# Waits kept per tile at pool borders, and images stored once for gathers by rows of taps

## The chip, the cores and the metric

The kernel runs on one core of one Trainium2 chip. The metric is the device time of the whole program in microseconds (us). Three runs of the kernel before took 10018.24, 10019.67 and 10020.51 us; the median is 10019.67. A profile is one execution recorded by the hardware profiler. Its engines are PE (matrix multiplication; PEld is its loading of weights), DVE (vector), ACT (activation functions), POOL (general) and SP, which here issues the data transfers (DMAs). Each engine works through its own list of instructions in order and waits on semaphores where an instruction needs another engine's work or a DMA.

## The reference

The input is 4 images of 128 channels and 64 x 64 pixels, float32. Four layers, each added to its input, follow a normalization:

```python
x = x + L0(_gn(x))      # two depthwise convolutions, patch order, selective scan
x = x + L1(_gn(x))      # 3 x 3 convolution, 128 to 128 channels
t = tokens(x)
t = t + L2_attn(_ln_t(t));  t = t + L2_ffn(_ln_t(t))   # 16 heads of 8, softmax; 64 experts
t = t + L3_attn(_ln_t(t));  t = t + L3_ffn(_ln_t(t))   # linear attention; 64 experts
```

Layer 0 begins with the part that the change touches. A depthwise convolution has one 3 x 3 filter for each channel:

```python
feat = _gelu(_dwconv2d(x, conv1_w, conv1_b))
ca = sigmoid(relu(feat.mean((2, 3)) @ ca1_w.T) @ ca2_w.T)
feat = _gelu(_dwconv2d(feat * ca[:, :, None, None], conv2_w, conv2_b))
scores = 0.7 * sigmoid(head(feat)) + 0.3 * sigmoid(10 * var(x, axis=1))
idx = argsort(-patch_mean(scores))          # 256 patches of 4 x 4 pixels
```

The pixels are put in that order of patches, a position code is added, and the sequence of 4096 tokens goes through a normalization, a projection to 256 channels, a causal convolution, and a scan with 16 states per channel (h = dA * h + dBx, y = sum of h * C). The result is projected back and put back in image order.

## The kernel before

**Layers 0 and 1** (`layers01`, from L268). `in_order(b)` prepares image b: it loads it, normalizes it by groups (`groupnorm_fill`, ACT at L216) into `xp`, a 66 x 66 image with a border of zeros, and runs the first depthwise convolution into `fp`, the second over `fp`, then scores, sort and the ordered sequence. Depthwise convolutions run on PE (`convolved`, whose matmuls carry the line L91 of the helper `mm`). One product takes 96 rows: 32 channels times the three vertical taps ky, so that PE sums the vertical taps, and three products at shifted columns sum the horizontal ones. Four groups of 32 channels make a chunk of 8 image rows. The rows of `under`, the operand, are channel and ky: SBUF holds channels on partitions, so the image goes through DRAM. `stored` (L443) writes it to `image_d`, with three copies of each channel shifted by one row, and `gather` (L453) reads a chunk's 96 x 4 rows with one DMA of 792 KB. `image_d[0]` takes `xp` and `image_d[1]` takes `fp`, each in two halves, one half being 12 DMAs of 264 KB. `staged` starts a chunk's gather a set number of turns ahead of its product (`first`), and each `under` has two buffers.

Image 0 is prepared alone. Then `scan` goes through 32 chunks of the four sequences, 16 slots each, and takes one turn of the other work per slot: `in_order(1)` beside image 0's scan and so on, and beside the last one the putting back and layer 1's convolution (`end`). A slot has on DVE a product (L900) and two scans (L911), on ACT two exponentials (L907, `decay`), on POOL the product with C (L915, `hs<-hs,c_sb`), and SP loads C for it (L869, `c_sb<-c_d`). The order of the instructions on all five engines is the one that the program writes (`manual_schedule`); `later` puts an instruction at the end of the turn. `conv` results are read by ACT (gelu, L130), in order with `decay`.

In the sort, two comparisons per image need a mask of which patch comes before which; it is computed anew each time (L581, DVE).

**Layer 2** (`layer2_attention`, L1103). For each image: `prepare` (head features, queries, keys, values through DRAM), `attention` (scores on PE, exponential on ACT at L1534, sums and products on PE, DVE and POOL), then `feed_forward`, which runs beside the next image's `prepare` and ends with the stores `xd<-x` (L1667). Attention ends with the store of `around_d` (L1436), and feed_forward begins with the load of `den` (L1567). Then x is loaded (L2072); **`expert_ffn`** (L1700, gate first: `gateT`, `gate_ps`), **`layer3_attention`** (L1928, first product `ln_xc`) and `expert_ffn` again follow, and x is stored.

**Pools.** Tiles come from pools that are opened and closed with `with`: layer 2 opens `l2_mid` and `l2_ps` for prepare and feed_forward, closes them, and opens `l2_work`, `l2_pssc`, `l2_psctx`, `l2_psacc` for attention, on the same bytes. When a pool is opened on bytes of closed ones, its first use waits for all users of those pools, engines and DMAs. All DMAs named here are issued by SP in program order.

Of the kernel before, what the change touches and what calls it, by code (L numbers as in the profile page):

```python
# [9 lines left out]
F32 = mybir.dt.float32  # L10
# [3 lines left out]
ALU = mybir.AluOpType  # L14
AX = mybir.AxisListType
PSUM = bass.MemoryType.PSUM
# [253 lines left out]
def layers01(K, xd, dpool, w, w1):  # L270
# [7 lines left out]
    SLOTS = 2 * NG  # L278
    TURNS_END = 53
    with ExitStack() as ctx:  # L280
        pool = lambda name, bufs, **kw: ctx.enter_context(tc.tile_pool(name=name, bufs=bufs, **kw))
        cst = pool("l0_const", 1)
        big = pool("l0_big", 1)
        small = pool("l0_small", 1)
# [138 lines left out]
        def in_order(b, made, work, psum):  # L423
# [10 lines left out]
            sm = small.tile([P, 256], F32, name="sm")  # L434
            unders, kept, squares, features, xls = {}, {}, {}, {}, {}

            def stored(img, i, half):


                n = HW // 2 * (HW + 2)  # L440
                for g in range(4):
                    for ky in range(3):
                        nc.sync.dma_start(  # L443
                            out=image_d[i][g, 32 * ky : 32 * ky + 32, n * half : n * half + n],
                            in_=img[32 * g : 32 * g + 32, HW // 2 * half + ky : HW // 2 * (half + 1) + ky, :].rearrange(
                                "p y x -> p (y x)"
                            ),
                        )
# [118 lines left out]
            def sort():  # L567
                yield from wait(6)
                sp = K.bank(psum, [P, 256], "sm_ps")
                mm(sp, share.to_broadcast([P, P]), sm)  # L570
                later(nc.vector.tensor_copy, sm, sp)
                yield from wait(2)
                beats = []
                for h in range(2):
                    dg = small.tile([P, P], F32, name="dg")
                    nc.vector.tensor_tensor(dg, sm[:, h * P : (h + 1) * P], K.ident, ALU.mult)
                    cl = small.tile([P, 1], F32, name="cl")
                    nc.vector.tensor_reduce(cl, dg, AX.X, ALU.add)

                    before = small.tile([P, 256], F32, name="before")  # L580
                    nc.vector.scalar_tensor_tensor(before, K.col, K.row[:, h : h + 1], ones256, ALU.is_gt, ALU.mult)  # L581
                    eq = small.tile([P, 256], F32, name="eq", tag="rank_eq")
                    nc.vector.scalar_tensor_tensor(eq, sm, cl, before, ALU.is_equal, ALU.mult)
                    bt = small.tile([P, 256], F32, name=f"beats{h}")
                    nc.vector.scalar_tensor_tensor(bt, sm, cl, eq, ALU.is_lt, ALU.add)
                    beats.append(bt)
                    yield
                yield
                rp = K.bank(psum, [P, 256], "rank_ps")
                for h in range(2):  # L590
# [438 lines left out]

        seqs = []  # L1030
        with (
            tc.tile_pool(name="l0_first", bufs=2) as work,
            tc.tile_pool(name="l0_ps", bufs=8, space=PSUM) as psum,
        ):
            for K.slot, _ in enumerate(in_order(0, seqs, work, psum)):
                K.flush()
            K.flush()
        with (
            tc.tile_pool(name="l0_prep", bufs=1) as prep,
            tc.tile_pool(name="l0_scan", bufs=2) as work,  # L1040
            tc.tile_pool(name="l0_ps", bufs=3, space=PSUM) as psum,
            tc.tile_pool(name="l0_psbc", bufs=1, space=PSUM) as psbc,
            tc.tile_pool(name="l0_psex", bufs=2, space=PSUM) as psex,
            tc.tile_pool(name="l0_psy", bufs=1, space=PSUM) as psy,
            tc.manual_schedule(
                engines={
                    mybir.EngineType.PE,
                    mybir.EngineType.DVE,
                    mybir.EngineType.Activation,
                    mybir.EngineType.Pool,  # L1050
                    mybir.EngineType.SP,
                }
            ),
        ):
# [11 lines left out]
        with (  # L1066
            tc.tile_pool(name="l0_last", bufs=2) as work,
            tc.tile_pool(name="l0_ps", bufs=8, space=PSUM) as psum,
        ):
            for _ in end(NB - 1, seqs[NB - 1], work, psum):  # L1070
                K.flush()
# [32 lines left out]
def layer2_attention(K, xd, dpool, w):  # L1104
# [4 lines left out]
    BT = NTT // NJ  # L1109
    scale = 1.0 / math.sqrt(HD)  # L1110
    with ExitStack() as ctx:
        pool = lambda name, bufs, **kw: ctx.enter_context(tc.tile_pool(name=name, bufs=bufs, **kw))
        cst = pool("l2_const", 1)
        keep = pool("l2_keep", 2)

# [39 lines left out]
        with tc.tile_pool(name="l2_ps0", bufs=1, space=PSUM) as ps0:  # L1155
# [516 lines left out]
        past = None  # L1672
        for b in range(NB + 1):
            with (
                tc.tile_pool(name="l2_big", bufs=1) as big,
                tc.tile_pool(name="l2_two", bufs=2) as two,
            ):
                with (
                    tc.tile_pool(name="l2_mid", bufs=2) as work,
                    tc.tile_pool(name="l2_ps", bufs=8, space=PSUM) as psum,  # L1680
                ):
                    parts = list(feed_forward(b - 1, past, work, psum)) if b > 0 else []
                    if b < NB:
# [4 lines left out]
                    break  # L1688
                past = keep.tile([P, NTT, NH], F32, name="dsum")
                with (  # L1690
                    tc.tile_pool(name="l2_work", bufs=2) as work,
                    tc.tile_pool(name="l2_pssc", bufs=3, space=PSUM) as pssc,
                    tc.tile_pool(name="l2_psctx", bufs=1, space=PSUM) as psctx,
                    tc.tile_pool(name="l2_psacc", bufs=1, space=PSUM) as psacc,
                    tc.manual_schedule(
                        engines={mybir.EngineType.PE, mybir.EngineType.DVE, mybir.EngineType.Pool}
                    ),
# [4 lines left out]
def expert_ffn(K, xs, w, tag):  # L1702
# [8 lines left out]
    NG = NE // GE  # L1711
    NHC = HID // P
    with ExitStack() as ctx:
        pool = lambda name, bufs, **kw: ctx.enter_context(tc.tile_pool(name=f"{tag}_{name}", bufs=bufs, **kw))
        cst = pool("const", 1)
        wts = pool("wts", 2)
        tok = pool("tok", 1)
# [209 lines left out]
def layer3_attention(K, xs, w):  # L1927
# [1 line left out]
    nc, tc, mm = K.nc, K.tc, K.mm  # L1929
    HD = 16  # L1930
    with ExitStack() as ctx:
        pool = lambda name, bufs, **kw: ctx.enter_context(tc.tile_pool(name=name, bufs=bufs, **kw))
        cst = pool("l3_const", 1)
        big = pool("l3_big", 2)
        work = pool("l3_work", 2)
# [119 lines left out]
@with_exitstack  # L2055
def kernel(ctx: ExitStack, tc: tile.TileContext, w: dict, out: bass.AP):
    nc = tc.nc
    cpool = ctx.enter_context(tc.tile_pool(name="const", bufs=1))
    dpool = ctx.enter_context(tc.tile_pool(name="dram", bufs=1, space=bass.MemoryType.DRAM))
    K = Common(tc, cpool)  # L2060

    def of(prefix):
# [5 lines left out]
    xpool = ctx.enter_context(tc.tile_pool(name="x", bufs=1))  # L2068
    xs = []
    for b in range(NB):  # L2070
        t = xpool.tile([P, L], F32, name=f"x{b}")
# [61 lines left out]
```

## Time and profile before

| | before |
|---|---|
| three runs, median | 10019.67 us |
| the profiled execution | 10014.33 us |
| its span, first to last instruction | 10012.5 us |
| PE busy | 8755.8 us (87%) |
| DVE busy | 7222.2 us (72%) |
| ACT busy | 7414.1 us (74%) |
| POOL busy | 4804.1 us (48%) |
| granted PE clock, mean | 0.916 |
| bytes by DMA | 669.38 MB, 67 GB/s |

Times in the profile count from the span's start. Roughly: 0 to 241 us prepares image 0, to 2740 is the scan, to about 2980 the end of layer 1 and layer 2's beginning, to about 8890 layer 2, to 9261 its experts, to 9649 layer 3's attention, then its experts. A busy share over the whole span is an average over these stages; the prediction therefore goes by stages. A line of a timeline shows start, length, engine, line of the kernel and operation, output and inputs, count, and in brackets how long the engine was idle before and what ended it. A line of the waits shows who waited, for what, the total, how many times, and the longest. On SP a DMA's length is that of its issue, not of the transfer; SP also stands at a DMA when the queue behind it is full.

### The profile page before, as it was taken

What the parts mean: (1) busy time and instruction counts of PE and PEld (TensorE: products, weight loads), DVE (VectorE), ACT (ScalarE), POOL (GpSimd) and SP (SyncE); (2) the same over time, 40 slices, a digit from 0 to 9 for tenths busy, and PEclk for the clock granted to TensorE, in tenths of its full rate; (3) what the DMA queues carried; (4) which work ended last, traced back from release to release, by engine and by line L of the source; (5) the groups of instructions that cost most, each with busy time, mean ns of one, the idle gap of its engine ahead of it and who ended that gap; (6) DMA issues with size and microseconds to landing.
All of it is one profiled execution on the core that took longest, in us unless ns stands there. A gap on an engine that the chain in (4) does not pass through costs nothing.

```text
span 10012.5 us, 187862 instructions
## 1 busy us (share of the span) xinstructions
PE 8755.8 (87%) x74074; PEld 3353.2 (33%) x74074; DVE 7222.2 (72%) x7883; ACT 7414.1 (74%) x10669; POOL 4804.1 (48%) x3175
## 2 busy tenths in 40 slices
PE   5687888889859999979999979999979999967767
PEld 1122222235433333333333333333333333323433
DVE  1779797998738888848888858888758888743463
ACT  2666766654439999969999969999969999941531
POOL 0567586775525555545555545555545555420000
PEclk9787887889979999989999989999989999978888
DMA  5634536222221211141211141211141111133004
GB/s 127 150 88 101 134 79 152 69 73 81 74 70 37 41 39 39 30 115 38 39 39 39 29 115 39 39 38 39 29 115 39 38 39 39 33 100 118 2 18 152
DMA packets 578291, 669.38 MB, mean 67 GB/s; under 512 B 113592, under 2 KB 369664, under 8 KB 570240
## 3 DMA queue, kind: packets, MB, share of 16 engines
q1 hardware_dynamic: 577408, 657.36, 27.1%
q8 instruction: 584, 9.57, 0.4%
q14 instruction: 299, 2.45, 0.1%
HBM read 446.84 MB, written 143.13 MB: 59 GB/s over the span
## 4 chain that ended last, share of the span: by engine, by line
PE 45%; DVE 4%; DMA 2%; ACT 2%; POOL 1%; issue 1%; SPq 1%; DVEq 0%; POOLq 0%; ACTq 0%
PE ctx_ps L91 20%; PE acc_ps L91 10%; PE score L91 8%; PE ln_xc L91 1%; DMA w<-in_L_ffn_weight 1%; PE ln_var L91 1%; PE hid_ps L91 1%; PE kv L91 1%; PE tok_t L1829 0%; PE ln_var L121 0%; PE pool L91 0%; PE ans_ps L91 0%; DVE ctx L1468 0%; PE o_ps L91 0%; SPq L1210 0%
## 5 line engine op out<-in xcount | busy, mean ns | idle before, releaser
L1534 ACT ACTIVATE ex<-score 128x1024 f32<-128x1024 f32 x5120 | 4927.9, 1037 | 176.0 <-PE score L91 90.2
L91 PE MATMUL ctx_ps<-ex,qt 128*32 128x512 f32 x20480 | 2736.5, 606 | 19.8 <-DVE ctx L1468 19.8
L1483 POOL TENSOR_TENSOR folded<-ex 128x1024 f32<-128x1024 f32 x512 | 1224.2, 2391 | 2124.0 <-ACT ex L1534 1866.1
L1540 DVE STREAM_TRANSPOSE turned<-ex 128x1024 f32<-128x1024 f32 x1536 | 1885.9, 1228 | 351.5 <-ACT ex L1534 279.1
L1516 DVE STREAM_TRANSPOSE turned<-ex 128x1024 f32<-128x1024 f32 x1532 | 1843.0, 1203 | 0.0
L91 PE MATMUL acc_ps<-turned,turned_v 128*32 128x256 f32 x24576 | 1769.4, 379 | 3.0 <-DVE turned L1546 3.0
L911 DVE TENSOR_TENSOR_SCAN hs<-decay,carry,hs 128x512 f32<-128x512 f32 x1024 | 1245.8, 1266 | 248.2 <-ACT decay L907 234.9
L91 PE MATMUL score<-queries,keys 32*128 32x512 f32 x10240 | 1333.6, 497 | 64.4 <-POOL queries L1218 35.8
L91 PEld LDWEIGHTS acc_ps<-turned,turned_v 128*32 128x32 f32 x24576 | 800.8, 110 | 1476.5 <-issue 1327.2
L915 POOL TENSOR_TENSOR hs<-hs,c_sb 128x1024 f32<-128x1024 f32 x512 | 1207.5, 2358 | 108.9 <-DMA c_sb<-c_d 66.5
L907 ACT ACTIVATE decay<-dt,a_neg 128x512 f32<-128x512 f32 x1024 | 693.0, 689 | 662.5 <-DVE hs L911 653.0
L91 PEld LDWEIGHTS score<-queries,keys 32*128 32x128 f32 x10240 | 512.1, 182 | 1160.4 <-ACT ex L1534 801.8
L1346 POOL TENSOR_TENSOR turned_v<-v,quarter 128x1024 f32<-128x1024 f32 x256 | 612.5, 2393 | 266.3 <-PE acc_ps L91 221.8
L91 PE MATMUL y_ps<-hs,pair 128*64 128x512 f32 x2048 | 664.0, 776 | 27.0 <-POOL hs L915 26.9
L1484 POOL TENSOR_TENSOR quarters<-folded 128x512 f32<-128x512 f32 x512 | 658.0, 1285 | 40.1
L91 PEld LDWEIGHTS ctx_ps<-ex,qt 128*32 128x32 f32 x20480 | 406.5, 108 | 655.4 <-issue 599.3
L900 DVE TENSOR_TENSOR hs<-dtx,b_ps 128x2048 f32<-128x2048 f32 x256 | 580.5, 2267 | 55.1 <-PE b_ps L91 29.8
L91 PE MATMUL b_ps<-dbc,state 32*64 32x512 f32 x1024 | 339.6, 745 | 224.5 <-DVE hs L900 224.4
L1534 ACT ACTIVATION_READ_ACCUMULATOR ex<-score 128x1 f32 x2048 | 437.7, 214 | 0.0
L914 POOL COPY carry<-hs 128x2 f32<-128x2 f32 x512 | 98.1, 192 | 700.1 <-DVE hs L911 673.9
L1468 DVE COPY ctx<-ctx_ps 128x512 f32<-128x512 f32 x256 | 176.9, 691 | 329.2 <-PE ctx_ps L91 323.5
L91 PE MATMUL conv<-under,deep 96*32 96x512 f32 x1536 | 217.9, 708 | 136.6 <-DMA under<-image_d 128.3
(371 smaller groups left out, 9156.9 us busy)
## 6 DMA issues: line engine op xcount, KB each, us to landing
c_sb<-c_d SPq DMA_DIRECT2D x512, 128.0 KB
queries<-head_d SPq DMA_DIRECT2D x1024, 64.0 KB
keys<-head_d SPq DMA_DIRECT2D x1024, 64.0 KB
under<-image_d SPq DMA_DIRECT2D x64, 792.0 KB
dt<-dt SPq DMA_DIRECT2D x128, 256.0 KB
dtx<-dtx SPq DMA_DIRECT2D x128, 256.0 KB
v<-value_d SPq DMA_DIRECT2D x1024, 32.0 KB
w<-in_L_ffn_weight SPq DMA_DIRECT2D x32, 1024.0 KB
```

The costliest lines, as they stand in the source:

```text
L91: self.nc.tensor.matmul(out, lhsT, rhs, start=start, stop=stop)
L900: nc.vector.tensor_tensor(hs, dtx2, bb.unsqueeze(1).to_broadcast([P, NQ, CH]), ALU.mult)
L907: nc.scalar.activation(ex, dt2[:, q, :], AF.Exp, scale=a_neg[:, q, g : g + 1])
L911: nc.vector.tensor_tensor_scan(hs[:, q, :], decays[q - 2 * i], hs[:, q, :], carry[:, g, q : q + 1], ALU.mult, ALU.add)
L915: nc.gpsimd.tensor_tensor(hs[:, two, :], hs[:, two, :], cs.unsqueeze(1).to_broadcast([P, 2, CH]), ALU.mult)
L1346: nc.gpsimd.tensor_tensor(t, v.unsqueeze(2).to_broadcast([P, 4 * BT, 4, HD]), quarter.unsqueeze(1).to_broadcast([P, 4 * BT, 4, HD]), ALU.mult,
L1468: nc.vector.tensor_copy(u, cps)
L1483: nc.gpsimd.tensor_tensor(hs, exs[:, :, 0], exs[:, :, 1], ALU.add)
L1484: nc.gpsimd.tensor_tensor(qs, hs[:, :, 0 : CH // 2], hs[:, :, CH // 2 :], ALU.add)
L1516: nc.vector.transpose(*upright)
L1534: nc.scalar.activation(ex, sps[p], AF.Exp, scale=scale, accum_out=sums[:, t : t + 1] if summed else None)
L1540: nc.vector.transpose(*upright)
```

## The change

There are three edits.

1. Every pool is opened with `reuse_waits="tile"`. A tile on reused bytes then waits for the users of earlier tiles on its own bytes (in PSUM, its own bank) and not for all users of the closed pools. Outside layer 0 the instructions and their order on each engine stay the same.
2. `image_d` holds the bordered image once: 128 channels of 66 x 66. `stored` writes a quarter of it (17, 16, 16 and 17 rows) with one DMA from 128 partitions, and `gather` takes three DMAs of 264 KB, one per ky, each to 32 partitions. Per image that is 8 stores and 48 gathers in place of 48 and 16, and 2.23 MB written for each of `xp` and `fp` in place of 6.49 MB. Quarters of `xp` are stored after fills 3, 5 and 7 and after the last, those of `fp` after every second chunk.
3. The two masks of the sort are computed once, at setup.

In the diff only pools of one kind are shown once; all the others get the same argument.

```diff
     SLOTS = 2 * NG
     TURNS_END = 53
     with ExitStack() as ctx:
-        pool = lambda name, bufs, **kw: ctx.enter_context(tc.tile_pool(name=name, bufs=bufs, **kw))
+        pool = lambda name, bufs, **kw: ctx.enter_context(tc.tile_pool(reuse_waits="tile", name=name, bufs=bufs, **kw))
         cst = pool("l0_const", 1)
         big = pool("l0_big", 1)
         small = pool("l0_small", 1)
 ...
         state = cst.tile([32, DS], F32, name="state")
         nc.vector.tensor_scalar(state, K.col[0:32, 8 : 8 + DS], row32[0:32], None, ALU.is_equal)
         c_d = dpool.tile([2, DS, CH], F32, name="c_d")
-        image_d = [dpool.tile([4, 96, HW * (HW + 2)], F32, name=f"image_d{i}") for i in range(2)]
+        image_d = [dpool.tile([P, (HW + 2) * (HW + 2)], F32, name=f"image_d{i}") for i in range(2)]
         y_d = [dpool.tile([P, L], F32, name=f"y_d{b}") for b in range(NB - 2)]
 
         pair = cst.tile([P, 64], F32, name="pair")
 ...
         deep2 = depthwise(w["conv2_w"], "deep2")
         rect = lambda t: t.rearrange("p (y x) -> p y x", x=HW)
         ones256 = K.ones[:, 0:1].to_broadcast([P, 256])
+        befores = [small.tile([P, 256], F32, name=f"before{h}", bufs=1) for h in range(2)]
+        for h in range(2):
+            nc.vector.tensor_scalar(befores[h], K.col, K.row[:, h : h + 1], None, ALU.is_gt)
 
         def image(b):
             t = big.tile([P, L], F32, name="xb", tag="mid")
 ...
             sm = small.tile([P, 256], F32, name="sm")
             unders, kept, squares, features, xls = {}, {}, {}, {}, {}
 
-            def stored(img, i, half):
-
-
-                n = HW // 2 * (HW + 2)
-                for g in range(4):
-                    for ky in range(3):
-                        nc.sync.dma_start(
-                            out=image_d[i][g, 32 * ky : 32 * ky + 32, n * half : n * half + n],
-                            in_=img[32 * g : 32 * g + 32, HW // 2 * half + ky : HW // 2 * (half + 1) + ky, :].rearrange(
-                                "p y x -> p (y x)"
-                            ),
-                        )
+            def stored(img, i, q):
+
+
+                lo, hi = 16 * q + 1 if q else 0, 16 * q + 17 if q < 3 else HW + 2
+                nc.sync.dma_start(
+                    out=image_d[i][:, lo * (HW + 2) : hi * (HW + 2)], in_=img[:, lo:hi].rearrange("p y x -> p (y x)")
+                )
 
             def gather(i, c):
                 n = 8 * (HW + 2)
                 t = unders[c] = work.tile([96, 4, n], F32, name="under", bufs=2)
-                nc.sync.dma_start(out=t, in_=image_d[i][:, :, n * c : n * c + n].rearrange("g q f -> q g f"))
+                for ky in range(3):
+                    at = (8 * c + ky) * (HW + 2)
+                    nc.sync.dma_start(
+                        out=t[32 * ky : 32 * ky + 32],
+                        in_=image_d[i][:, at : at + n].rearrange("(g q) f -> q g f", q=32),
+                    )
 
             def even():
                 while K.slot % 2:
 ...
 
             for c in range(NCH):
                 fill(c)
-                if c == 6:
-                    stored(xp, 0, 0)
+                if c in (3, 5, 7):
+                    stored(xp, 0, c // 2 - 1)
                 yield
             fp = kept["fp"] = big.tile([P, HW + 2, HW + 2], F32, name="fp", tag="mid")
             nc.gpsimd.memset(fp[:, 0, :], 0.0)
 ...
             nc.gpsimd.memset(fp[:, 1 : HW + 1, 0:1], 0.0)
             nc.gpsimd.memset(fp[:, 1 : HW + 1, HW + 1 : HW + 2], 0.0)
             yield
-            stored(xp, 0, 1)
+            stored(xp, 0, 3)
 
             def first_stored(c):
-                if c in (4, 7):
-                    stored(fp, 1, c // 5)
+                if c % 2:
+                    stored(fp, 1, c // 2)
 
             yield from even()
             yield from staged(NCH, 2, lambda c: gather(0, c), None, None, first, None, first_stored)
 ...
                     cl = small.tile([P, 1], F32, name="cl")
                     nc.vector.tensor_reduce(cl, dg, AX.X, ALU.add)
 
-                    before = small.tile([P, 256], F32, name="before")
-                    nc.vector.scalar_tensor_tensor(before, K.col, K.row[:, h : h + 1], ones256, ALU.is_gt, ALU.mult)
                     eq = small.tile([P, 256], F32, name="eq", tag="rank_eq")
-                    nc.vector.scalar_tensor_tensor(eq, sm, cl, before, ALU.is_equal, ALU.mult)
+                    nc.vector.scalar_tensor_tensor(eq, sm, cl, befores[h], ALU.is_equal, ALU.mult)
                     bt = small.tile([P, 256], F32, name=f"beats{h}")
                     nc.vector.scalar_tensor_tensor(bt, sm, cl, eq, ALU.is_lt, ALU.add)
                     beats.append(bt)
 ...
             with (
-                tc.tile_pool(name="l2_big", bufs=1) as big,
-                tc.tile_pool(name="l2_two", bufs=2) as two,
+                tc.tile_pool(reuse_waits="tile", name="l2_big", bufs=1) as big,
+                tc.tile_pool(reuse_waits="tile", name="l2_two", bufs=2) as two,
             ):
 ...
```

More of the change, by code (lines that the diff above doesn't have):

```diff
@@ L1031, in layers01 @@
         with (
-            tc.tile_pool(name="l0_first", bufs=2) as work,
-            tc.tile_pool(name="l0_ps", bufs=8, space=PSUM) as psum,
+            tc.tile_pool(reuse_waits="tile", name="l0_first", bufs=2) as work,
+            tc.tile_pool(reuse_waits="tile", name="l0_ps", bufs=8, space=PSUM) as psum,
         ):
@@ L1038, in layers01 @@
         with (
[L1039 to L1044, printed above, removed]
+            tc.tile_pool(reuse_waits="tile", name="l0_prep", bufs=1) as prep,
+            tc.tile_pool(reuse_waits="tile", name="l0_scan", bufs=2) as work,
+            tc.tile_pool(reuse_waits="tile", name="l0_ps", bufs=3, space=PSUM) as psum,
+            tc.tile_pool(reuse_waits="tile", name="l0_psbc", bufs=1, space=PSUM) as psbc,
+            tc.tile_pool(reuse_waits="tile", name="l0_psex", bufs=2, space=PSUM) as psex,
+            tc.tile_pool(reuse_waits="tile", name="l0_psy", bufs=1, space=PSUM) as psy,
             tc.manual_schedule(
@@ L1066, in layers01 @@
         with (
-            tc.tile_pool(name="l0_last", bufs=2) as work,
-            tc.tile_pool(name="l0_ps", bufs=8, space=PSUM) as psum,
+            tc.tile_pool(reuse_waits="tile", name="l0_last", bufs=2) as work,
+            tc.tile_pool(reuse_waits="tile", name="l0_ps", bufs=8, space=PSUM) as psum,
         ):
@@ L1111, in layer2_attention @@
     with ExitStack() as ctx:
-        pool = lambda name, bufs, **kw: ctx.enter_context(tc.tile_pool(name=name, bufs=bufs, **kw))
+        pool = lambda name, bufs, **kw: ctx.enter_context(tc.tile_pool(reuse_waits="tile", name=name, bufs=bufs, **kw))
         cst = pool("l2_const", 1)
@@ L1154, in layer2_attention @@
         nc.vector.tensor_copy(biases[:, 1:2], b2)
-        with tc.tile_pool(name="l2_ps0", bufs=1, space=PSUM) as ps0:
+        with tc.tile_pool(reuse_waits="tile", name="l2_ps0", bufs=1, space=PSUM) as ps0:
             bp = ps0.tile([P, 2], F32, name="bias_ps")
@@ L1674, in layer2_attention @@
             with (
-                tc.tile_pool(name="l2_big", bufs=1) as big,
-                tc.tile_pool(name="l2_two", bufs=2) as two,
+                tc.tile_pool(reuse_waits="tile", name="l2_big", bufs=1) as big,
+                tc.tile_pool(reuse_waits="tile", name="l2_two", bufs=2) as two,
             ):
                 with (
-                    tc.tile_pool(name="l2_mid", bufs=2) as work,
-                    tc.tile_pool(name="l2_ps", bufs=8, space=PSUM) as psum,
+                    tc.tile_pool(reuse_waits="tile", name="l2_mid", bufs=2) as work,
+                    tc.tile_pool(reuse_waits="tile", name="l2_ps", bufs=8, space=PSUM) as psum,
                 ):
@@ L1690, in layer2_attention @@
                 with (
[L1691 to L1694, printed above, removed]
+                    tc.tile_pool(reuse_waits="tile", name="l2_work", bufs=2) as work,
+                    tc.tile_pool(reuse_waits="tile", name="l2_pssc", bufs=3, space=PSUM) as pssc,
+                    tc.tile_pool(reuse_waits="tile", name="l2_psctx", bufs=1, space=PSUM) as psctx,
+                    tc.tile_pool(reuse_waits="tile", name="l2_psacc", bufs=1, space=PSUM) as psacc,
                     tc.manual_schedule(
@@ L1713, in expert_ffn @@
     with ExitStack() as ctx:
-        pool = lambda name, bufs, **kw: ctx.enter_context(tc.tile_pool(name=f"{tag}_{name}", bufs=bufs, **kw))
+        pool = lambda name, bufs, **kw: ctx.enter_context(tc.tile_pool(reuse_waits="tile", name=f"{tag}_{name}", bufs=bufs, **kw))
         cst = pool("const", 1)
@@ L1931, in layer3_attention @@
     with ExitStack() as ctx:
-        pool = lambda name, bufs, **kw: ctx.enter_context(tc.tile_pool(name=name, bufs=bufs, **kw))
+        pool = lambda name, bufs, **kw: ctx.enter_context(tc.tile_pool(reuse_waits="tile", name=name, bufs=bufs, **kw))
         cst = pool("l3_const", 1)
@@ L2057 @@
     nc = tc.nc
-    cpool = ctx.enter_context(tc.tile_pool(name="const", bufs=1))
-    dpool = ctx.enter_context(tc.tile_pool(name="dram", bufs=1, space=bass.MemoryType.DRAM))
+    cpool = ctx.enter_context(tc.tile_pool(reuse_waits="tile", name="const", bufs=1))
+    dpool = ctx.enter_context(tc.tile_pool(reuse_waits="tile", name="dram", bufs=1, space=bass.MemoryType.DRAM))
     K = Common(tc, cpool)
@@ L2067 @@
     layer2_attention(K, xd, dpool, of("L2_attn_"))
-    xpool = ctx.enter_context(tc.tile_pool(name="x", bufs=1))
+    xpool = ctx.enter_context(tc.tile_pool(reuse_waits="tile", name="x", bufs=1))
     xs = []
```

## The prediction

> **What bounds the kernel now.** I read the page first. It shows an execution of 10014.33 us with a span of 10012.5, so 1.8 us lie around the span; the median of the runs, 10019.67, is 5.3 above it. I sum against 10014.33 and add the 5.3 at the end. PE is the busiest at 87%, but the average hides stages, so the busy time by windows comes next (columns: length, then busy time of PE, PEld, DVE, ACT, POOL, clock, DMA share, GB/s):
>
> ```profile
> 0.00:241.00 241.00, 123.60 (x654) 45.48 (x654) 35.58 (x102) 64.53 (x100) 24.90 (x41) 0.91 0.54 132
> 1000.00:1200.00 200.00, 158.93 (x717) 43.15 (x718) 139.61 (x109) 142.77 (x184) 114.23 (x85) 0.87 0.69 155
> 1200.00:2740.00 1540.00, 1300.96 (x4572) 520.14 (x4570) 1321.06 (x1122) 899.85 (x1219) 1039.87 (x787) 0.85 0.35 87
> ```
>
> In the first 241 us (image 0 alone) no engine is busy more than half. In the scan DVE is the fullest, but in the stretch with an image's convolutions it drops to 70%. The list of waits names what is missing:
>
> ```profile
> DVE hs L911 <- ACT decay L907: 234.9, 106, 18.1
> ...
> PE conv L91 <- DMA under<-image_d: 128.3, 17, 40.6
> ```
>
> Then the timeline. Image 0 (SPq is SP issuing DMAs; the bracket is idle time before a line and what ended it):
>
> ```profile
> 35.45 27.89 SPq L443 DMA_DIRECT2D image_d<-xp  x24
> ...
> 72.37 7.95 PE L91 MATMUL conv<-under,deep 96*32 96x512 f32 x48 [40.63 <-DMA under<-image_d]
> ...
> 98.70 12.44 SPq L443 DMA_DIRECT2D image_d<-fp  x11
> ...
> 120.45 5.23 PE L91 MATMUL conv<-under,deep 96*32 96x512 f32 x24 [11.67 <-DMA under<-image_d]
> ```
>
> PE waits for 24 stores, later for 12 more that sit ahead of two gathers on SP. In the scan the same stores hold a gather, PE and ACT wait, and DVE stands:
>
> ```profile
> 480.86 13.74 SPq L443 DMA_DIRECT2D image_d<-fp  x12
> ...
> 505.52 5.35 PE L91 MATMUL conv<-under,deep 96*32 96x512 f32 x24 [10.68 <-DMA under<-image_d]
> ...
> 515.09 2.46 DVE L911 TENSOR_TENSOR_SCAN hs<-decay,carry,hs 128x512 f32<-128x512 f32 x2 [18.11 <-ACT decay L907]
> ```
>
> Last, a border between pools: prepare to attention of layer 2, where the scores are done at 4468.2 but the exponential's table waits for a store that the old pool's tiles had:
>
> ```profile
> 4466.63 1.52 PE L91 MATMUL score<-queries,keys 32*128 32x512 f32 x6 [1.06 <-issue]
> 4466.70 4.42 SPq L1667 DMA_DIRECT2D xd<-x  x3
> ...
> 4473.17 1.28 ACT L1534 ACT_TABLE_LOAD   x1 [8.51 <-DMA xd<-x]
> ```
>
> **What the Trainium skill says.** "SBUF — State Buffer", Door 1: The DMA port swizzle: partitions 0 to 31 reach 8 of 16 ports, about 218 GB/s at best, 128 partitions all 16. The 24 old stores, 32 partitions each, took 1.16 us per 264 KB, 233 GB/s: near it, slightly over. So the new stores on 128 partitions should be no slower per byte. "DMA: Bandwidth & Descriptors", Anatomy of one DMA: about 2.0 us fixed, mostly the receipt; so a chain store, then gather, pays it twice however few the bytes. The trace has a gather issued at 77.8 and used at 83.58. "SBUF — State Buffer", two separate sides: a DVE operation with two SBUF inputs and a GpSimd one that reads SBUF lock each other out for a whole instruction; used for the masks below, and the trace agrees.
>
> **First image.** Out go 24 stores of xp (6.49 MB) and their two-step wait, in come 4 stores (2.23 MB) of which the first gather needs one. The fills of xp end at 38.2 (ACT L216, 32.47 + 5.75). Stores are issued from about 35 to 39; 2.23 MB at the old 233 GB/s is 9.6 us, so all have landed by about 47, the first quarter earlier; with 5 us for a gather, convolution starts near 50 instead of 72.37: 22 us. The second term: pairs of chunks start 10.2 us apart (83.58, 93.80), limited by gathers. Four pairs, and some 4 us for fp stores between them, end near 95; now they end at 125.7. That is 30. The wait of 4.09 before a chunk of the second convolution (148.86) goes too, since its gathers need quarters long stored. The rest, up to the scan, moves along whole: **34 us**. If three gathers of 264 KB cost 1 us more per chunk than one of 792 KB, 8 us of it are lost: low end 26. If quarters are faster on 16 ports and pairs at 9 us, 40.
>
> **Convolutions in the scan.** Images 1 to 3 are prepared beside the scan, in an order written by slots. Eleven waits for gathers there (5.77, 2.36, 10.68, 5.46, 1.96, 0.61, 6.60, 11.20, 4.47, 1.49, 11.44) make 62.0 us; with image 0's they are the 128.3 of the list. After, a store is one issue and SP is free; a gather is issued three slots, some 13 us, ahead of its use, so even 8 us of flight is hidden. DVE can only get back what it lost: for each wait the lesser of it and the DVE stall behind it (9.15, 2.27, 18.11, 8.58, 3.62, 16.87, 7.89, 18.11): 5.77 + 2.27 + 10.68 + 5.46 + 3.62 + 11.20 + 4.47 + 11.44 = 54.9. What remains of the 18.11, about 7.4, is a chunk of matmuls (5.35) and table loads on ACT (1.28 each), untouched. POOL's waits for c_sb (9.42 at 499.56, 10.73, 11.70) lie in the same stretches and are not counted twice.
>
> The masks: six `before` operations in the scan take 2.51 to 2.55 us each on DVE, two for image 0 about 0.47. But the one at 629.92 ends at 632.43, just after POOL's multiply (629.81, 2.34): it stands in the lock. Without it `eq`, also with two SBUF inputs, comes at that moment and waits as long. So I take 6 × 0.48 = 2.9 from the scan (high end 15, the full six), and 2 × 0.45 added at setup against 2 × 0.47 removed: nothing. Scan: **57 us**. Low end 40: a third of the stalls merely move to the next late thing. High end 75.
>
> SP's issues per image go from 48 stores and 16 gathers to 8 and 48. Removed stores block SP for 13.5 us per dozen; added gathers cost 0.31 to 0.5 us each, 16 × 2 × 0.4 = 13 us per image, spread over 16 turns, 0.8 us ahead of a c_sb load that POOL uses two slots later: hidden; without that cover, 3 × 13 = 39 us.
>
> **Borders.** Program order on PE, ACT and POOL is the same outside layer 0, so only waits change; each is priced by what then ends last.
> - Prepare to attention, images 1 to 3: the first exponential comes at 4474.46. PE has nothing behind 4465.57 (the end of ln_var, 4464.92 + 0.65) and the queries are cast by 4465.45, so scores can begin there and, with the table loaded before, the first exponential comes near 4466.2: 8.2 us earlier, 7.9 after a little for POOL's later first sums. Next late: v loads, which stay behind the xd stores on SP (4472.98, about 1 us earlier); their turned copies (two of 2.35) end near 4480.1, the accumulation wants them at 4482. 3 × 7.9 = 23.7; if v is later than that, 3 × 5. Image 0 (2978.13) waits for the queries' cast, data: only the table load, 1.3.
> - Attention to feed_forward, four times: the den load was issued at 5765.10, the store of around_d before it at 5763.05 (0.34); SP is in order, so it can come at 5763.4. 4 × 1.7 = 6.8.
> - Layer 2 to experts: x loads at 8889.88, possible at 8888.05: 1.7. Experts to layer 3: ln_xc at 9263.71 waits for the last clearing on DVE, needed about 9261.9: 1.8. Layer 3 to experts: gateT issued at 9649.33, gate_ps at 9654.17 after 5.70 idle for it; the last x comes at 9649.25: 4.9. Layer 1 to 2: theta already sits behind xd stores on SP: 0.
>
> Sum: **40 us** (25 to 48).
>
> **Total.** 34 + 57 + 40 = 131. 10014.3 − 131 = 9883 on the profile's own scale, 10019.67 − 131 = 9889 against the runs.
>
> **Rivals.**
> - *Moved stalls.* The scan's stalls have a second cause just behind (24 matmuls in 5.35 us where the same take 2.78 at 519.08, ACT table loads, c_sb) and give only half; v loads are late at the borders. For it: 7.4 of 18.1 remains anyway, and DVE's total wait on decay is 234.9, of which convolutions explain a third. 28 + 30 + 22 = 80: about 9940. Chance 0.22.
> - *More comes free.* All of the stalls with convolutions (82 after the eight, so 82 in place of 55) and all mask time come back, faster quarters: 40 + 82 + 43 = 165: about 9855. Against it: table loads are data, and the lock passes on. Chance 0.13.
> - *The tile waits give nothing.* SP and the engines are in order, so a looser wait may leave the same last one, as at layer 1 to 2. Then 34 + 57 = 91: about 9929. Against it: the 8.51 before the table load has no data behind it. Chance 0.12.
> - *Slower.* Gathers on 32 partitions use 8 ports at a time and pay three landings. If one of 64 chunk gathers takes over 13 us plus 131/64 = 2.0, about 15 us in place of 5.8, the gain is gone; at 18 us, 64 × 3 over that gives about 10210. Against: the gather on 96 partitions also sends two thirds through the same 8 even ports, so its port time is unchanged. Chance 0.04.
>
> **Numbers.** The forecast has 0.49. A difference under 0.2% (20 us) can't be told from none here. Faster 0.94, within 0.2% 0.02, slower 0.04. The range takes in three rivals and the bounds of the terms: 9850 to 9950; 9889 is the likeliest.
>
> **What would show it.** Image 0's first convolution near 50 us and the scan's first DVE work 34 earlier; no wait of PE for `under` over 2 us in the scan; stalls like the one at 515 shrunk to 7; DVE near 95% around image 1's convolutions; no ACT wait for the xd store in layer 2, and first exponentials 8 us sooner after the scores. Wrong if waits for `under` stay (gather too slow or stores still ahead), if `eq` shows no 2.5 us, or if PE waits for `turned_v` or `v` after a border.

## The result

The changed kernel takes 9883.69 us (median of four runs, 9868.94 to 9902.87), where the kernel before took 10020.09 on the same chip: a ratio of 0.9861, 95% interval 0.9840 to 0.9882. In a second comparison it was 0.9869 (0.9854 to 0.9884). The forecast was 9889.

The profiled execution is one of 9881.09 us with a span of 9879.3, 133.2 us shorter than before. To see where they go, the start of the same instruction in two traces, each counted from its span's start, is subtracted. This table does it for the profile of before, the changed kernel, a second profile of the changed kernel, and four kernels of the experiments below. It shows how much later (or, negative, earlier) than before each kernel reaches the mark:

| first instruction of | before, us | changed | changed, again | tiles alone | image alone | stored thrice | gathers twice |
|---|---|---|---|---|---|---|---|
| first convolution | 72.4 | -27.4 | -24.7 | +0.3 | -27.0 | -2.3 | -24.0 |
| the scan | 278.2 | -43.8 | -43.4 | +0.8 | -42.3 | -8.4 | -29.2 |
| the scan's last group | 2725.8 | -98.5 | -90.3 | +7.6 | -83.0 | -30.8 | -69.2 |
| exponentials of image 0 | 2979.4 | -97.5 | -88.3 | +6.2 | -81.4 | -30.9 | -68.0 |
| exponentials of image 1 | 4474.5 | -106.4 | -98.1 | -3.8 | -82.6 | -40.6 | -77.1 |
| exponentials of image 3 | 7464.8 | -127.0 | -118.8 | -24.5 | -82.9 | -61.3 | -97.8 |
| layer 3's products (kv) | 9270.7 | -132.7 | -118.1 | -29.5 | -80.2 | -67.1 | -102.7 |
| the last stores | 9990.5 | -133.2 | -114.7 | -27.9 | -76.5 | -66.9 | -99.9 |

So 44 us come from image 0, 55 from the scan and 35 from what lies behind it (from the second profile 43, 47 and 24).

The windows of the changed kernel that answer to those shown of before, with the same columns:

```profile
0.00:197.00 197.00, 120.89 (x654) 46.59 (x654) 35.42 (x102) 64.27 (x100) 24.71 (x41) 0.91 0.47 119
933.00:1120.00 187.00, 158.70 (x705) 42.56 (x698) 142.30 (x111) 143.65 (x185) 116.75 (x86) 0.86 0.63 144
1120.00:2641.00 1521.00, 1292.39 (x4570) 517.94 (x4566) 1318.09 (x1117) 898.83 (x1218) 1038.35 (x786) 0.86 0.32 83
```

The work in each stage is nearly the same, done in less time. The second window lies around image 2's convolutions: DVE's share there is 76%, up from 70. Around image 1's (340 to 530 us) it is 75%. DVE's waits for `decay` and PE's for gathers:

```profile
DVE hs L912 <- ACT decay L908: 180.1, 108, 7.2
...
PE conv L91 <- DMA under<-image_d: 36.4, 11, 13.6
```

PE's waits for gathers fall from 128.3 to 36.4 us, and in the scan alone from 62.0 to 10.5. DVE's waits for `decay` fall by 54.8. The timeline of image 0:

```profile
33.62 4.51 SPq L444 DMA_DIRECT2D image_d<-xp  x4
...
44.93 8.33 PE L91 MATMUL conv<-under,deep 96*32 96x512 f32 x48 [13.62 <-DMA under<-image_d]
56.07 7.05 PE L91 MATMUL conv<-under,deep 96*32 96x512 f32 x48 [2.81 <-DMA under<-image_d]
...
75.31 8.49 PE L91 MATMUL conv<-under,deep 96*32 96x512 f32 x48 [3.33 <-DMA under<-image_d]
```

The four stores are issued in 4.51 us (27.89 before). The convolution begins at 44.93 and ends at 83.80 (125.7 before). In the scan, the place of the stall of 18.11:

```profile
433.71 0.99 SPq L444 DMA_DIRECT2D image_d<-fp  x1
...
445.31 2.78 PE L91 MATMUL conv<-under,deep 96*32 96x512 f32 x24 [0.57 <-DMA under<-image_d]
...
452.30 2.46 DVE L912 TENSOR_TENSOR_SCAN hs<-decay,carry,hs 128x512 f32<-128x512 f32 x2 [3.92 <-ACT decay L908]
```

The store is one issue, the gather's wait is 0.57, and the 24 products take 2.78 in place of 5.35: PE had stood idle 0.57 us before them and not 10.68, and its granted clock in them is 1.00, where it was 0.50 in those of the kernel before. DVE's stall is 3.92. The border from prepare to attention:

```profile
4366.57 1.28 ACT L1535 ACT_TABLE_LOAD   x1
...
4367.40 0.67 PE L91 MATMUL score<-queries,keys 32*128 32x512 f32 x2
4368.11 3.02 ACT L1535 ACTIVATE ex<-score 128x1024 f32<-128x1024 f32 x3 [0.25 <-PE score L91]
4368.38 1.59 PE L91 MATMUL score<-queries,keys 32*128 32x512 f32 x6 [0.31 <-DVE ln_kept L125]
4368.60 4.45 SPq L1668 DMA_DIRECT2D xd<-x  x3
```

The table is loaded while the scores are still on their way, and the exponential comes before the stores that it waited for, not after them.

### The profile page after: what moved, and what is told of

It reads as the page before. It is cut to its first block, busy times and chain, and to the rows that moved or that the text cites. A ratio compares the mean times of both kernels' runs of the same rounds, so it can differ in the third digit from the quotient of the medians.

```text
span 9879.3 us, 187787 instructions
## 1 busy us (share of the span) xinstructions
PE 8736.1 (88%) x74074; PEld 3348.6 (34%) x74074; DVE 7220.5 (73%) x7877; ACT 7410.6 (75%) x10669; POOL 4802.8 (49%) x3175
## 4 chain that ended last, share of the span: by engine, by line
PE 69%; DVE 10%; POOL 6%; ACT 5%; DMA 4%; issue 3%; SPq 2%; DVEq 0%; POOLq 0%; ACTq 0%
PE ctx_ps L91 27%; PE acc_ps L91 13%; PE score L91 11%; PE conv L91 4%; DVE hs L912 3%; POOL hs L916 3%; PE ln_xc L91 2%; PE y_ps L91 2%; DVE hs L901 2%; PE xc_ps L91 1%; DMA w<-in_L_ffn_weight 1%; PE ln_var L91 1%; PE b_ps L91 1%; PE hid_ps L91 1%; PE kv L91 1%
## 5 line engine op out<-in xcount | busy, mean ns | idle before, releaser
L1535 ACT ACTIVATE ex<-score 128x1024 f32<-128x1024 f32 x5120 | 4925.4, 1036 | 218.5 <-PE score L91 125.7
L916 POOL TENSOR_TENSOR hs<-hs,c_sb 128x1024 f32<-128x1024 f32 x512 | 1207.3, 2358 | 81.4 <-DMA c_sb<-c_d 40.3
L915 POOL COPY carry<-hs 128x2 f32<-128x2 f32 x512 | 98.1, 192 | 673.4 <-DVE hs L912 652.0
L1526 DVE TENSOR_REDUCE dacc<-quarters 128x2 f32<-128x512 f32 x508 | 327.1, 644 | 0.0
```

The costliest lines, as they stand in the source:

```text
L916: nc.gpsimd.tensor_tensor(hs[:, two, :], hs[:, two, :], cs.unsqueeze(1).to_broadcast([P, 2, CH]), ALU.mult)
L1526: nc.vector.tensor_reduce(at, qs, AX.X, ALU.add)
L1535: nc.scalar.activation(ex, sps[p], AF.Exp, scale=scale, accum_out=sums[:, t : t + 1] if summed else None)
```

## The experiments

### One edit at a time

`tile_only` is the kernel before with every `tile_pool(` given the new argument and nothing else.

> Only edit 1 (tile waits everywhere); stores, gathers and masks as before. Theory: the borders alone, 35 us less than before (the trace of the changed kernel has 35 of its 133 after the scan's end), about 9985, with the three exponentials of layer 2 each 8 earlier after their scores, and the first 2700 us as before within 2. Rival 'the tile waits give nothing' (SP and the engines are in order): 10020. Rival 'part of the first 98 us is from waits at the pools of layer 0': more than 50 less.

It took 9978.23 us, ratio 0.9948 (0.9931 to 0.9965). Its column in the table is flat to the scan's start, wanders by 7 us in the scan, and then gains at the borders: 8.25 us at each of the three from prepare to attention, about 1 to 1.5 at each from attention to feed_forward, 5.0 at layer 3 to the last experts. Its list of waits has no more entry of ACT for `xd<-x`, which in the kernel before is

```profile
ACT L1534 <- DMA xd<-x: 25.5, 3, 8.5
```

So the tile waits do give the borders, and nothing that the trace shows in layers 0 and 1. By the runs the gain is 52 us, with an interval of 35 to 69, where 35 was expected and 28 stands in the table; the profiled execution was the slowest of the four. The runs alone would not exclude the rival with the pools of layer 0, since their middle is over its 50; the flat start of the column does for image 0, and in the scan the column shows a loss.

`image_only` is the kernel before with the new `image_d`, `stored` and `gather`, the old waits and masks computed each time.

> Only edit 2 (image stored once in quarters, three gathers); old waits, masks computed each time. Theory: 44 from image 0 and 52 from the scan, 96 less than before, about 9924; the borders of layer 2 as before. If the parts need each other (a late store hidden by a border wait), the two kernels with one edit do not add up to 136 within 15.

It took 9934.93 us, 0.9908 (0.9893 to 0.9923): 42 us at the scan's start, 41 more in the scan, the borders as before (-82.6, -83.0, -82.9 at the exponentials). This is as expected. In ratios, 0.0052 and 0.0092 make 0.0144, the changed kernel has 0.0139 and 0.0131: within the intervals the parts add up.

`tile_attention` puts the argument on four pools only:

```diff
-                    tc.tile_pool(name="l2_work", bufs=2) as work,
+                    tc.tile_pool(reuse_waits="tile", name="l2_work", bufs=2) as work,
 ...    # and l2_pssc, l2_psctx, l2_psacc
```

> The kernel before, with the tile waits on the four pools of layer 2's attention alone. Theory: the three borders from prepare to attention, 8.2 each with images 1 to 3, 25 of the 35 that the tile waits give in all; nothing at attention to feed_forward, at the experts and in layer 3. Rival (the exponential waited for something else that all pools together removed): 0 at those borders.

It took 9998.88 us, 0.9970 (0.9958 to 0.9983). A border is best measured from the end of the queries' copy, the last work ahead of it, to the first exponential. First the kernel before at image 1, then this kernel:

```profile
4463.56 1.89 POOL L1218 CAST queries<-queries 128x2048 fp32r<-128x2048 f32 x1
...
4474.46 2.85 ACT L1534 ACTIVATE ex<-score 128x1024 f32<-128x1024 f32 x3
```

```profile
4464.69 1.89 POOL L1218 CAST queries<-queries 128x2048 fp32r<-128x2048 f32 x1
...
4467.34 2.07 ACT L1534 ACTIVATE ex<-score 128x1024 f32<-128x1024 f32 x2 [0.26 <-PE score L91]
```

That is 9.01 and 0.76 us, and so it is at all three borders: 9.01 or 9.02 in each trace with the old waits there, 0.76 to 0.79 in each with the new. Three times 8.25 is 24.8, as expected. (From the end of one attention to the next exponential this kernel gained 9.2, 6.7 and 6.4, since the work between wanders by 1 to 2 us.) At attention to feed_forward it gains nothing on SP, as the prediction had it; first this kernel, then `tile_only`:

```profile
5755.46 0.34 SPq L1436 DMA_DIRECT2D around_d<-acc  x1
5757.51 0.31 SPq L1567 DMA_DIRECT2D den<-den_d  x1
```

```profile
5758.52 0.34 SPq L1436 DMA_DIRECT2D around_d<-acc  x1
5758.97 0.38 SPq L1567 DMA_DIRECT2D den<-den_d  x1
```

With the old wait 2.05 us pass between the two issues, with the new one 0.45.

### Bytes and issues, or quarters?

Edit 2 changes both how much is stored and when. Two kernels take them apart. `thrice` keeps the quarters and their times but stores each row three times again, 12 DMAs per quarter, and gathers with one DMA:

```diff
 ...    # image_d and gather as in the kernel before
-                nc.sync.dma_start(
-                    out=image_d[i][:, lo * (HW + 2) : hi * (HW + 2)], in_=img[:, lo:hi].rearrange("p y x -> p (y x)")
-                )
+                for g in range(4):
+                    for ky in range(3):
+                        a, e = max(0, lo - ky), min(HW, hi - ky)
+                        nc.sync.dma_start(
+                            out=image_d[i][g, 32 * ky : 32 * ky + 32, a * (HW + 2) : e * (HW + 2)],
+                            in_=img[32 * g : 32 * g + 32, a + ky : e + ky, :].rearrange("p y x -> p (y x)"),
+                        )
```

> The changed kernel, but each row stored three times again, 12 stores per quarter of the image, at the changed kernel's quarter times, and one gather of 792 KB per chunk. Theory (the bytes and the issues on SP hold the gathers): image 0's first convolution again near 70 us, waits for under again over 60 us in total, about 70 slower than the changed kernel, 9955. Rival (it was the time of storing, halves against quarters): at most 30 slower, 9914, waits in the scan gone.

It took 9946.80 us, 63 or 58 more than the two medians of the changed kernel. Image 0 is nearly as before, its scan starting 8.4 us earlier and not 44:

```profile
35.07 27.32 SPq L447 DMA_DIRECT2D image_d<-xp  x48
...
70.10 8.16 PE L91 MATMUL conv<-under,deep 96*32 96x512 f32 x48 [37.33 <-DMA under<-image_d]
```

Twice as many stores of half the size take the same 27 us, so it is the bytes that hold SP more than the count: in the kernel before the first three issues take 0.34 to 0.58 us and the later ones mostly about 1.3, and here the shorter half took about 0.42 each, at which 48 would make 20 us. These stores, as those of before, leave from 32 partitions; the image stored once from 32 partitions was not run, so what the spread over 128 gives apart from the bytes is an estimate only: 2.23 MB take 10.4 us at the 215 GB/s measured below and 6.1 at 368. In the scan the quarters do help while the bytes are many: the waits for `under` there are 26.7 us, between 62.0 and 10.5. `halves_once` is the other way round, stored once, in halves at the old times:

```diff
-                lo, hi = 16 * q + 1 if q else 0, 16 * q + 17 if q < 3 else HW + 2
+                lo, hi = (HW // 2 + 2, HW + 2) if q else (0, HW // 2 + 2)
 ...    # called after fill 6 and after the last; for fp after chunks 4 and 7
```

> The changed kernel, its image stored once but in two halves at the old times (one DMA each) in place of four quarters. Theory (bytes and issues ahead of the gathers on SP, not quarters): image 0's start of the scan at most 8 later than in the changed kernel, each image in the scan at most 4 more, so 0 to 20 slower, 9885 to 9905. Rival (quarters make the gain): 40 or more slower, waits of PE for under over 60 us in total.

9897.68 us, 14 or 9 more than the two medians of the changed kernel, with overlapping runs; the waits for `under` are 47.2 us in all, 20.8 in the scan; its scan starts 45.0 us earlier than before (the changed kernel's 43.8 and 43.4) and ends 88.7 earlier (98.5 and 90.3). Fewer bytes give nearly all; what quarters add on top of that is nothing in image 0 and lies within the scatter after it.

### The slack of a gather

`gathers_doubled` puts ahead of each of the three DMAs one of the same bytes into a buffer in DRAM:

```diff
+                spare = spare_d[c % 4]    # four buffers in DRAM
                 for ky in range(3):
                     at = (8 * c + ky) * (HW + 2)
+                    nc.sync.dma_start(
+                        out=spare[32 * ky : 32 * ky + 32],
+                        in_=image_d[i][:, at : at + n].rearrange("(g q) f -> q g f", q=32),
+                    )
```

> The changed kernel, and ahead of each of a gather's three DMAs one of the same bytes into a DRAM buffer that nobody reads: the gather's DMA work and issues doubled or more. Theory (13 us of slack in the scan, none in image 0): image 0 about 5 us longer per chunk for its 16 chunks where it is limited by gathers, so 30 to 60 later, and the scan no longer than in the changed kernel within 10: 9915 to 9945. Rival 'gathers are as late as before in the scan': the scan another 30 or more longer, 9960 and above, with waits of PE for under of 5 us and more in it.

It took 9914.24 us. Image 0 lost 14.6 us, half of the least expected, and the scan another 14.7, more than the 10 allowed and half of the rival's 30. Waits of PE for gathers in the scan:

```profile
PE conv L91 <- DMA under<-image_d: 25.6, 9, 5.5
```

So neither account holds as put: the slack in the scan is there but not the full 13 us everywhere, and image 0 is less bound by gathers than I thought. Doubling the gathers costs 31 or 25 us by the two medians of the changed kernel, under 0.5 for each of the 64; this bounds the rival in which they eat the gain.

### The masks

`masks_each_time` is the changed kernel without edit 3, `masks_only` the kernel before with edit 3 alone; `after_again` is the changed kernel on the same chip as these two.

> The changed kernel once more, for the same chip as the three below. 0.9861 of before within 0.002; in its trace 36 us of waits for under, and the same places as in its first profile, so that what differs between two profiles of one kernel is known.

> The changed kernel without edit 3: masks computed for each image. Theory (the lock passes on to eq): in the scan the operations before, eq and beats take 23.4 us in place of 19.8, so 3 to 4 us slower, not told apart by the median. Rival (the 15 that the masks show come back whole, as the 15 us between the scan's end in the changed kernel and in the one with edit 2 alone suggest): 12 to 16 slower at the scan's end.

> The kernel before with edit 3 alone. Theory (lock passes on): eq 2.4 us where before stood, the scan's end 3 to 4 us earlier. Rival: 12 to 16 earlier.

Medians: 9889.16 (0.9869), 9900.09 (0.9879, interval 0.9862 to 0.9895) and 10023.03 (1.0001, 0.9992 to 1.0009). The timeline of the changed kernel shows what happens at the second mask of image 1, DVE first, then POOL:

```profile
574.41 2.43 DVE L584 SCALAR_TENSOR_TENSOR eq<-sm,cl,before 128x256 f32<-128x256 f32 x1
576.87 0.49 DVE L586 SCALAR_TENSOR_TENSOR beats<-sm,cl,eq 128x256 f32<-128x256 f32 x1
```

```profile
574.20 2.35 POOL L916 TENSOR_TENSOR hs<-hs,c_sb 128x1024 f32<-128x1024 f32 x1
```

`eq`, 0.48 in the kernel before, takes 2.43 and ends just after POOL's product. Summed over the six masks in the scan, `before`, `eq` and `beats` take 23.4 us in the kernel before and in `masks_each_time`, and 19.8 in the changed kernel and in `masks_only`: 3.6 saved. The scan's end differs by 6.3 (`masks_each_time` against `after_again`) and 6.8 (`masks_only` against before, between its first group and its last), neither the 3 to 4 nor the 12 to 16 expected; but at the masks themselves, from 12 us ahead of them to 12 us behind, the traces of each pair part by 1.03 to 1.05 us per image, 3.1 in all, and the rest arises in places without masks. The next section shows such a place between two profiles of one kernel.

### A version beyond both, and what took its gain

In image 0 a gather waits until the product two chunks before it is done. `under4` gives image 0 four buffers:

```diff
-                t = unders[c] = work.tile([96, 4, n], F32, name="under", bufs=2)
+                t = unders[c] = work.tile([96, 4, n], F32, name="under", bufs=4 if b == 0 else 2)
```

> The changed kernel with four buffers of under for image 0 (two for the others). Theory (in image 0 a gather starts when the chunk two before it is done, and PE waits for its landing, 25.8 us in six waits, 13.6 of them for the first): without that the chunks of the first convolution are 1 us apart less, the scan starts 5 to 12 us earlier, 9875 or so. Rival (DMA rate or the stores of fp ahead of a gather on SP limit it): less than 3.

The scan starts 5.8 us earlier than in `after_again`, as expected, but at its end the two are level (-90.4 and -90.3), and the median, 9884.83, can't be told from 9889.16. The 5.8 are lost within 35 us early in image 0's scan, beside convolutions of image 1. The two profiles of the changed kernel part at the corresponding place one image later. There both are at the same work within a microsecond; first the window of the first profile, then of the second (the number after the five engines is the granted clock):

```profile
956.00:966.00 10.00, 10.00 (x48) 3.54 (x45) 9.48 (x9) 8.09 (x12) 5.11 (x4) 1.00 1.06 252
```

```profile
956.00:966.00 10.00, 10.00 (x41) 2.12 (x38) 7.99 (x8) 6.36 (x9) 5.08 (x4) 0.62 0.74 187
```

and the same eight products on PE in each:

```profile
956.38 1.94 PE L91 MATMUL y_ps<-hs,pair 128*64 128x512 f32 x8
```

```profile
958.40 3.68 PE L91 MATMUL y_ps<-hs,pair 128*64 128x512 f32 x8
```

With a clock of 0.62 over these 10 us (0.50 in the eight products themselves) PE is full and does less. DVE's next product stands for it, first in the first profile, then in the second:

```profile
969.21 2.29 DVE L901 TENSOR_TENSOR hs<-dtx,b_ps 128x2048 f32<-128x2048 f32 x1 [0.21 <-PE b_ps L91]
```

```profile
973.78 2.29 DVE L901 TENSOR_TENSOR hs<-dtx,b_ps 128x2048 f32<-128x2048 f32 x1 [2.84 <-PE b_ps L91]
```

Within 40 us the second profile falls 6 us behind, and it ends the scan 8 behind. So a stretch of the scan beside convolutions was worth 6 us more or less by the clock that PE had there. `under4` shows the same at its own place (a DVE wait of 2.84 for `b_ps`, where `after_again` has 0.22). How much of the scatter of the runs comes from such places was not counted. What decides the clock there wasn't settled: PE had stood idle 2.08 us just before in the second profile and not in the first, but a kernel that keeps PE busy there was not tried. Over the scans of all twelve traces idle time and slow products go together: all 36 groups of 24 products that came after an idle time of PE of over 3.6 us took 4.5 us or more, and of 446 that came after none about nine in ten took under 3.

## Why the prediction was right

The forecast was 5 us off, from terms that were off by more and partly cancelled: image 0 gave 10 more than forecast, the scan 2 or 10 less, the borders 5 or 16 less. The traces show the mechanism of each term, but for the exceptions named below; that the sum came so near is in part luck.

- **Image 0: 34 forecast, 44 measured.** The mechanism held in the main: the stores no longer keep the gathers waiting. That the first gather gains by needing one quarter only is not shown: SP issues it at 38.22, after all four stores, and `halves_once` starts its scan no later. The mis-sized term is the step "2.23 MB at the old 233 GB/s". DMA rates, from windows while only stores move, before (37 to 66 us) and after (35 to 40.5):

```profile
37.00:66.00 29.00, 0.00 (x0) 0.00 (x0) 0.00 (x0) 1.21 (x2) 0.51 (x4) 1.00 0.98 215
```

```profile
35.00:40.50 5.50, 0.00 (x0) 0.00 (x0) 0.00 (x0) 2.79 (x4) 0.77 (x5) 1.00 0.99 368
```

  215 GB/s from 32 partitions, 368 from 128. (The 233 came from the issue times on SP, which end before the last bytes have moved.) The new stores also have shorter rows, but those of `thrice`, with rows as short and from 32 partitions, ran at 231:

```profile
37.00:60.00 23.00, 0.00 (x0) 0.00 (x0) 0.00 (x0) 2.24 (x4) 0.51 (x4) 1.00 0.93 231
```

  This agrees with the page of the Trainium skill that the prediction cites ("SBUF — State Buffer", Door 1: The DMA port swizzle), 8 ports against 16; I used it only to say "no slower". The convolution started at 44.93, not near 50. The second mis-sized term: the 4 us for fp stores among the chunks; they cost nothing that the timeline shows. Pairs of chunks came 9.6 us apart (56.07, 65.70, 75.31) after a first gap of 11.1 in the first profile, and 10.3 and 10.4 apart after 11.0 in the second, where I had 10.2. Three gathers on 32 partitions are thus about as fast as one on 96. The wait of 4.09 in the second convolution went, but one of 2.79 came at the chunk ahead of it.
- **The scan: 57 forecast, 55 and 47 measured.** The sum of the smaller of each wait and the stall behind it, 54.9, is met by DVE's waits for `decay`, 54.8 less. That agreement is in part chance: in `image_only` the same waits fall by 56.2 and the scan gains 41, and place by place the sum does not hold. At the first stalled convolution of each image 8.0, 7.1 and 7.1 us came back and 4.9, 5.1 and 5.4 went again two slots later: in image 1 the next product waited 2.72 for its gather and took 5.35. At the second one, 14.2 and then 3.5 came back in image 1 and 12.0 and 14.8 in images 2 and 3, where I had 10.7, 11.2 and 11.4: without the idle time ahead of it the same product ran in 2.78. I had called the 5.35 untouched. (The eight stalls listed in the prediction sum to 84.6, not 82.) Two signs that I named did not come: DVE near 95% around image 1's convolutions (75%), and no wait for `under` over 2 us (five waits, 10.5 us, the longest 3.0). ACT's table loads and the products remain; the rival of moved stalls had this right, its sum (30) not.
- **The masks: 2.9 forecast, 3.6 in the operations' own time, 3.1 in the scan at their places.** That `eq` takes over the wait is confirmed to a tenth: 2.40 to 2.43 where `before` had 2.51 to 2.55. This agrees with the section of the Trainium skill that the prediction cites ("SBUF — State Buffer", two separate sides): in all twelve traces each of these six operations began while POOL's product ran and ended 0.28 or 0.29 us after it.
- **The borders: 40 forecast, 35 and 24 measured.** Prepare to attention: 8.25 each (7.9 forecast). Attention to feed_forward: 1.5, 1.5, 1.5 and 0.95 (1.7). Layer 3 to the last experts: 4.9 (4.9). Experts to layer 3: 3.2 (1.8). One term failed: image 0's first exponential saved its table load of 1.3, but its queries came later, so from the end of the scan to it 1.0 was lost. The rest of the gap lies elsewhere. The last experts, started 137 us earlier, ended 133 earlier: from their first `gate_ps` to the end the profile of the changed kernel has 362.5 us and that of the kernel before 358.3. But that 358.3 is the shortest of all twelve profiles: the others have 359.7 to 365.1, and `masks_only`, with the old waits and the old image, 363.5. So about 4 us of the shortfall belong to the one profile of before that all are measured against, and not to a border.
- **The rivals.** That the tile waits give nothing is refuted by `tile_only`, and the slower gather by the pairs, 9.6 to 10.4 us apart, and by `gathers_doubled`. That more comes free (165) overshoots; image 0 was beyond its own high end (44 against 40), the scan and the borders not.

## What to carry to other kernels

Transfers that sit on an in-order queue cost twice, once as bytes and once as a barrier for what is behind them: look first at what is issued between a producer and the load that it waits for, and store the data once even if that makes three loads of one. At the border of two buffer pools look for the wait that has no data behind it, and price each border by what is late next. Before a few microseconds are put down to a change, compare the length of that stage in several executions, and in kernels without the change. And when a stall is removed beside a full in-order chain, count also what the idle engine's lower clock had cost, in both directions.

## What the runs showed of the hardware beyond that

- Stores from 128 partitions ran at 368 GB/s, where the old ones from 32 ran at 215 and, with rows of half the length, at 231.
- Removing an operation that stands waiting for another engine (2.5 us) saves only its own 0.5 when the next one needs the same thing.
- The same eight products took 1.94 us at a clock of 1.00 and 3.68 at 0.50, in two executions of one program, at the same place.
